# Selective-scan layer of a four-layer kernel: output gate recomputed at the end, table loads written out, bf16 remainders through the matrix engine, partial sums copied into PSUM, convolution in single taps

## The chip, the cores and the metric

The kernel runs on one core of a Trainium2 chip. The metric is the device time of one launch in microseconds (us). A core has five instruction queues that run side by side and wait for each other by semaphores: PE (TensorE, matrix products; its weight loads are listed as PEld), DVE (VectorE), ACT (ScalarE), POOL (GpSimd) and SP (SyncE, which here issues all DMAs). Each queue is strictly in order: an instruction that waits holds up everything behind it on the same queue.

## The reference, cut to what matters

Four layers follow each other on `x` of shape (8, 64, 64, 64): a state-space layer (L0), two attention layers and a test-time-training layer. Only the scan part of L0 is touched by the change. For each of the 8 images, with 64 channels, 128 inner channels (DI), 16 states (N) and 4096 positions:

```python
xz = in_proj(layernorm(x))                 # 64 -> 2*128 channels
xi, z = split(xz)
xc = silu(dwconv3x3(xi))                   # depthwise, 9 taps
xs = [rows, columns, rows reversed, columns reversed] of xc      # K = 4 directions
dts, Bs, Cs = split(xproj_w[k] @ xs[k])    # 4 + 16 + 16 rows
dt = softplus(dtproj_w[k] @ dts + dtproj_b[k])
h[n] = h[n] * exp(dt * A[n]) + dt * Bs[n] * u                    # scan over 4096 positions
y[k] = sum_n h[n] * Cs[n] + D[k] * xs[k]
y = sum of the four directions, put back in row order
out = x + outproj(layernorm(y) * silu(z))
```

## The kernel before, in words

The scan layer (`scan_layer`) is one hand-ordered program (`tc.manual_schedule()`): the engines receive instructions in the order in which the Python code emits them. For each image there are 16 **steps** (4 directions k times 4 chunks of 1024 positions), and in each step 16 **units**, one for each state n: 2048 units in all. A unit is:

- `decay` (ACT, L733): `a = exp(dt * A[n])`, 128x1024.
- `spread` (PE, L751): the row `Bs[n]`, held as three bf16 pieces (`bs`, 48 rows), is broadcast over 128 partitions into the PSUM tile `z` by two bf16 matmuls with the weights `pick`. For n in `BY_POOL = (0, 3, 6, 8)` a DMA broadcasts the row instead (`bt`), POOL multiplies it by `dt*u` (`product`, L741) and ACT copies it into `z` (L748).
- `unit` (DVE): for the other twelve n, `z = z * dt*u` (L778); then `tensor_tensor_scan` gives `h` (L782); then POOL multiplies `ct = ct * h` (L787), where `ct` is `Cs[n]` broadcast by DMA into one of five buffers.
- `sum_up` (PE, L848): `ct` is added into the PSUM tile `yps` by an fp32 matmul with a 128x128 weight, the identity or, in the last quarter of an image, the centring matrix `lno_cen` (`ident - 1/128`).

The sum runs two to three units behind (`LAG`). At n = 3, `empty` copies the finished `yps` of the step before into `y` (ACT, L817) and `begin_sum` starts the new one: in the first four steps of an image with `skipd` times u, later with the partial sum `y` itself, read back through an fp32 matmul with identity or `lno_cen` (L839). In two steps of an image the sum stays in PSUM.

Everything else is **background**: items of the form (`make`, `use`) in one queue (`Background`). Each unit takes one item (`bg.before`): `make` issues its PE work at once, `bg.after` runs what `bg.later` put off and then the `use` of the item before. In the units 6, 7, 8 (`idle`) only items without `make` are taken. Background work is:

- the normalisation and input projection of the next image (`norm_x`), its convolution (`convolve`: nine fp32 diagonal matmuls for each 512 positions, cut into items of two taps, then Silu, L553), and its gate: `gate` computes `silu(z)` and stores it in DRAM (`zd`, L529, L530);
- the layer norm of the finished image (`norm_y`: squares, variances through DRAM in `inverse_root`, root, reciprocal, then `apply`: DVE multiplies y by the row of inverse roots, L460, and ACT applies gain and bias, L461); `load` brings `zd` back (L575), POOL multiplies it with y (`multiply`, L580), and `project_out` projects and adds x;
- for the next step: `project` (step sizes dt, rows B and C) and its softplus (`soft1` to `soft3`: Exp L653, Ln L656, POOL add L659), the POOL product `step_input` (L678), and `pieces`, which splits B into three bf16 pieces: ACT rounds (L691), POOL subtracts (L695), ACT rounds the rest (L698), POOL subtracts again (L701).

Activation tables are not mentioned in the kernel; where a function is not in the loaded table, the build puts an ACT_TABLE_LOAD before the instruction that needs it, so it is shown under that instruction's line.

Of the kernel before, what the change touches and what calls it, by code (L numbers as in the profile page):

```python
# [18 lines left out]
NB = 8  # L19
# [146 lines left out]
class Background:  # L166
# [24 lines left out]
    def before(self, busy=False, slots=0):  # L191
        self.now = None
        src = None
        if busy:
            if not self.queue or self.queue[0][0]:
                return
        elif self.open:
            if not self.first and (self.item or len(self.open) >= slots or not self.queue):
                src = self.open
        elif self.groups and self.credit and not self.first and slots >= len(self.groups[0]):  # L200
            src = self.open = self.groups.popleft()
            self.credit -= 1
        if src is None and self.queue:
            src = self.queue
            self.first = max(0, self.first - 1)
        self.item = src is not self.open
        if src:
            make, use = src.popleft()
            self.now = (use, make() if make else None)
# [32 lines left out]
def scan_layer(cm, x_in, w, xh):  # L242

    tc, nc = cm.tc, cm.nc
    with ExitStack() as ctx:
# [58 lines left out]
        skipd = cm.tile([DI, DI], "skipd")  # L304
        nc.vector.tensor_scalar(skipd, cm.ident, skip, None, ALU.mult)
# [11 lines left out]
        lno_cen, lno_avg = cm.norm_consts(DI, "lno")  # L317

        eps = cm.tile([128, 1], "eps")
        nc.vector.memset(eps, 1e-5)  # L320
        pick = cm.pool.tile([3 * N, N], BF16, name="pick", tag="pick")
# [4 lines left out]
        nc.vector.tensor_copy(pick, rows)  # L326
        pad = padp.tile([DI, S + 2, S + 2], F32, name="pad", tag="pad")
        nc.gpsimd.memset(pad, 0.0)
        bg = Background()

# [5 lines left out]
        def inverse_root(nb):  # L336
# [5 lines left out]
            def put(ps, n, at):  # L342
                t = work.tile([NBK, BK], F32, name="vrow", tag="rstd", bufs=1)
# [10 lines left out]
            def root(_):  # L354
                nc.scalar.activation(sm["v"], sm["v"], AF.Sqrt, bias=eps)

# [9 lines left out]
            chain += [(None, back), none, none, none]  # L366
            return put, chain, sm

        def norm_x(b, xn, pairs, project_in):
# [48 lines left out]
            for i in pairs:  # L418
                out += [project_in(2 * i), project_in(2 * i + 1)]
                if i + 2 in pairs:  # L420
                    out.insert(-1, apply(i + 2))
                if b:
                    out.append(none)
            return out

        def norm_y(y, blocks, load, multiply, project_out):
# [8 lines left out]
            def variance(j):  # L435
# [7 lines left out]
                def use(ps):  # L443
                    put(ps, 1, j - j0)
                    if j + 2 in blocks:
                        square(j + 2)

                return make, use

            def apply(j):  # L450
# [7 lines left out]
                def use(ps):  # L458
# [3 lines left out]
                    if j - 1 in blocks:  # L462
                        multiply(j - 1)
# [4 lines left out]
            for j in blocks:  # L468
                out.append(variance(j))
                if j in blocks[1:6:2] or nb == 2:  # L470
                    at = j if nb == 2 else j0 + (j - j0) // 2
                    out.append((None, lambda _, at=at: load(at)))
            out += chain
            out += [apply(j) for j in blocks[:2]]
            end = (None, lambda _: multiply(blocks[-1]))
            if nb == 2:
                out += [end, none]
            for j in blocks:
                if j + 2 in blocks:
                    out.append(apply(j + 2))  # L480
                    if j + 2 == blocks[-1]:
                        out.append(end)
                out += [project_out(j), none]
# [5 lines left out]
        def before(b):  # L489

            xn = io.tile([2 * C, NBK // 2, BK], F32, name="xn", tag="xn", bufs=1)
# [5 lines left out]
            zd = dr.tile([DI, L], F32, name="zd", tag="zd")  # L497
# [7 lines left out]
            def project_in(j):  # L505
# [11 lines left out]

                return make, use

            def gate(j):  # L520
                def make():
                    ps = bank("zps")
                    half, x = block(j)
                    nc.tensor.matmul(ps, win[half, 1, :], x, start=True, stop=True)
                    return ps

                def use(ps):
                    z = work.tile([DI, BK], F32, name="z", tag="z", bufs=3)
                    nc.scalar.activation(z, ps, AF.Silu, bias=inb[:, 1:2])  # L529
                    bg.later(lambda: nc.sync.dma_start(zd[:, bass.ts(j, BK)], z))  # L530
# [3 lines left out]
            def convolve(j):  # L534
# [17 lines left out]
                def use(_):  # L552
                    nc.scalar.activation(u[:, bass.ts(j, BK)], held[0], AF.Silu, bias=convb)  # L553
                    if b:
                        bg.done[b] += 1

                cuts = (0, 5, 9) if b == 0 else (0, 3, 5, 7, 9) if b == NB - 1 else (0, 2, 4, 6, 8, 9)
                parts = [(part(t0, t1), None) for t0, t1 in zip(cuts, cuts[1:])]
                return parts[:-1] + [(parts[-1][0], use)]
# [4 lines left out]
            return u, zd, items, [gate(j) for j in range(NBK)], [convolve(j) for j in range(NBK)]  # L564

        def after(b, y, zd, blocks=range(NBK)):
# [4 lines left out]
            def load(j):  # L571
                xr = work.tile([C, BK], F32, name="xr", tag="xr", bufs=3)
                nc.sync.dma_start(xr, xf[:, bass.ts(j, BK)])
                z = work.tile([DI, BK], F32, name="z", tag="z", bufs=3)
                nc.sync.dma_start(z, zd[:, bass.ts(j, BK)])  # L575
                gated[j] = (xr, z)

            def multiply(j):
                z = gated[j][1]
                nc.gpsimd.tensor_tensor(z, z, y[:, bass.ts(j, BK)], ALU.mult)  # L580

            def project_out(j):
                def make():
                    po = bank("ops")
                    xr, z = gated[j]
                    nc.tensor.matmul(po[:C], cm.ident[:C, :C], xr, start=True, stop=False)
                    nc.tensor.matmul(po[:C], wout, z, start=False, stop=True)
# [12 lines left out]
            return norm_y(y, blocks, load, multiply, project_out)  # L600
# [80 lines left out]
        def pieces(ctl, low):  # L681
# [33 lines left out]
            return ([fetch, first, subtract, second, third, store] if ctl["k"] < 2 else []) + [get]  # L715
# [108 lines left out]
        def begin_sum():  # L824
# [8 lines left out]
            if ctl["new_y"]:  # L833
                wt, so = skipd, ordered(ctl["u"], ctl["k"], ctl["c"])
            else:
                mine = ("row", "col")[ctl["k"] % 2]
                wt, so = ctl["mat"], own(layout(ctl["b"], mine), ctl["c"])
            for i in range(CH // BK):
                nc.tensor.matmul(  # L839
                    ctl["ps"][:, bass.ts(i, BK)].rearrange("p (a b) -> p a b", b=S),  # L840
                    wt, so[:, i * half : (i + 1) * half, :], start=True, stop=False,
                )

        def sum_up():

            ctl, n, ct = pending.popleft()
            for i in range(CH // BK):
                nc.tensor.matmul(  # L848
                    ctl["ps"][:, bass.ts(i, BK)], ctl["mat"], ct[:, bass.ts(i, BK)],
# [19 lines left out]
        def prepare(b, s):  # L869
# [10 lines left out]
            if b == 0 and s < NCH:  # L880
# [6 lines left out]
                mat=lno_cen if s >= 3 * NCH - 1 else cm.ident,  # L887
            )
            ctl["pieces"] = pieces(ctl, low)
# [6 lines left out]
        def start(b):  # L896
            u, zd, items, gates, convs = before(b)
            images[b] = {"u": u, "zd": zd}
            bg.add(items[0] + items[1])
            if b == 0:  # L900
# [3 lines left out]
                later[NCH] = gates  # L904
            else:
                bg.done[b] = 0
                bg.add([(None, lambda _: bg.groups.extend(deque(conv) for conv in convs))])
                bg.add(gates)


        with tc.manual_schedule():
            start(0)
# [14 lines left out]
            for b in range(NB):  # L927
                for s in range(4 * NCH):
# [7 lines left out]
                    bg.credit = 2 if b == NB - 2 else 1  # L936
                    idle = () if early or late else (6, 7, 8)
                    hooks = {}
                    if nxt:
# [6 lines left out]
                        else:  # L946
                            hooks = {14 - len(do) + i: [f] for i, f in enumerate(do)}
# [10 lines left out]
                    for n in range(N):  # L958
# [30 lines left out]
                        if s == 0 and n == LAG + 2 and b > 0:  # L989
                            last = images.pop(b - 1)  # L990
                            bg.add(after(b - 1, last["row"], last["zd"]))
                            bg.add([(None, lambda _, b=b - 1: bg.flushed.add(b))])
                        if late and n == LAG + 2:
                            c = 4 * NCH - s
                            bg.add(after(b, images[b]["row"], images[b]["zd"], range(2 * c, 2 * c + 2)))
                        if s == (1 if b else NCH) and n == 0 and b + 1 < NB:
                            bg.add(later.pop(NCH, []))
# [10 lines left out]
            bg.add(after(NB - 1, last["row"], last["zd"], range(2)))  # L1008
# [1149 lines left out]
```

## Time and profile before

| | us |
|---|---|
| median of 3 runs | 12334.72 |
| lowest, highest | 12313.69, 12336.37 |
| the profiled execution itself | 12328.75 |
| its span, first to last instruction | 12326.7 |
| scan layer up to the first scan | 94.4 |
| the 2048 units of the scan layer | 94.4 to 7018.6 |
| of these, images 1 to 6 | 1015.2 to 6153.7 |
| end of the scan layer's last stores | about 7053.6 |

All numbers of the profile belong to one profiled execution. Starts of images and steps are read from the scan instructions, 16 to a step and 256 to an image. A row of a group gives busy time, mean duration in ns of one instruction, then the idle time of that engine just before it and what ended the idle time. The matrix engine's instructions overlap: an fp32 matmul is two records of about 0.6 us each, but back to back one starts every 0.43 us.

### The profile page before, as it was taken

What the parts mean: (1) busy time and instruction counts of PE and PEld (TensorE: products, weight loads), DVE (VectorE), ACT (ScalarE), POOL (GpSimd) and SP (SyncE); (2) the same over time, 40 slices, a digit from 0 to 9 for tenths busy, and PEclk for the clock granted to TensorE, in tenths of its full rate; (3) what the DMA queues carried; (4) which work ended last, traced back from release to release, by engine and by line L of the source; (5) the groups of instructions that cost most, each with busy time, mean ns of one, the idle gap of its engine ahead of it and who ended that gap; (6) DMA issues with size and microseconds to landing.
All of it is one profiled execution on the core that took longest, in us unless ns stands there. A gap on an engine that the chain in (4) does not pass through costs nothing. (4 is left out here: it accounts for less than half of the span.)

```text
span 12326.7 us, 120038 instructions
## 1 busy us (share of the span) xinstructions
PE 11203.1 (91%) x38827; PEld 4075.9 (33%) x38827; DVE 10359.2 (84%) x7334; ACT 7820.8 (63%) x10409; POOL 7399.3 (60%) x3510
## 2 busy tenths in 40 slices
PE   7899999999999999999998899999987779999999
PEld 2233332332332332333322233232335463333333
DVE  5999999999999999999999776868677686676767
ACT  4776776776766766767766554646547574555554
POOL 5999999999999999999999700000006480000000
PEclk8999999999999999999999899999998789999999
DMA  3666666666666666666666400000011100000000
GB/s 115 207 213 218 209 209 217 219 203 216 218 210 213 211 210 217 213 215 213 199 213 211 164 24 26 5 25 7 17 41 41 41 21 24 19 4 19 5 11 6
DMA packets 541331, 1562.16 MB, mean 127 GB/s; under 512 B 127360, under 2 KB 144400, under 8 KB 538128
## 3 DMA queue, kind: packets, MB, share of 16 engines
q1 hardware_dynamic: 540688, 1554.36, 38.5%
q8 instruction: 309, 5.06, 0.2%
q14 instruction: 334, 2.74, 0.1%
HBM read 1456.41 MB, written 88.87 MB: 125 GB/s over the span
## 5 line engine op out<-in xcount | busy, mean ns | idle before, releaser
L787 POOL TENSOR_TENSOR ct<-ct,h 128x1024 f32<-128x1024 f32 x2048 | 4794.6, 2364 | 248.2 <-DVE h L782 113.3
L782 DVE TENSOR_TENSOR_SCAN h<-a,state,z 128x1024 f32<-128x1024 f32 x1536 | 3573.1, 2342 | 118.2 <-ACT z L748 67.1
L1159 DVE TENSOR_TENSOR sum<-sum,ex 128x1024 f32<-128x1024 f32 x1920 | 2347.5, 1223 | 618.1 <-ACT ex L1152 484.4
L1152 ACT ACTIVATE ex<-sc 128x1024 f32<-128x1024 f32 x2048 | 1968.1, 1024 | 1359.6 <-PE sc L1147 1359.6
L848 PE MATMUL yps<-ct,ident 128*128 128x512 f32 x5632 | 2809.0, 630 | 2.5 <-POOL ct L787 2.4
L733 ACT ACTIVATE a<-dt,amat 128x1024 f32<-128x1024 f32 x2048 | 2345.4, 1147 | 725.9 <-DVE h L782 712.5
L778 DVE TENSOR_TENSOR z<-z,e 128x1024 f32<-128x1024 f32 x1536 | 1863.3, 1213 | 221.1 <-PE z L751 143.2
L1166 PE MATMUL av<-ex,v 128*64 128x512 f32 x8192 | 1950.0, 604 | 0.0
L1147 PE MATMUL sc<-q,k 16*128 16x512 f32 (+1 forms) x8192 | 1562.2, 623 | 4.2 <-ACT q L1140 3.1
L848 PEld LDWEIGHTS yps<-ct,ident 128*128 128x128 f32 x5632 | 1006.4, 194 | 1384.2 <-issue 1220.6
L751 PE MATMUL z<-bs,pick 48*128 48x512 bf16 x3072 | 948.0, 389 | 536.5 <-DVE h L782 485.5
L848 PE MATMUL yps<-ct,lno_cen 128*128 128x512 f32 x2560 | 1276.3, 630 | 0.0
L782 DVE TENSOR_TENSOR_SCAN h<-a,z 128x1024 f32<-128x1024 f32 x512 | 1162.7, 2282 | 81.4 <-ACT z L748 57.2
L741 POOL TENSOR_TENSOR bt<-bt,e 128x1024 f32<-128x1024 f32 x512 | 1210.1, 2364 | 5.3 <-DMA bt<-bc 5.3
L1473 POOL TENSOR_TENSOR gt<-gt,pad 128x1024 f32<-128x1024 f32 x16 | 34.9, 2179 | 1570.2 <-ACT gt L1472 1570.2
L1166 PEld LDWEIGHTS av<-ex,v 128*64 128x64 f32 x8192 | 512.2, 136 | 1332.8 <-issue 1278.9
L1147 PEld LDWEIGHTS sc<-q,k 16*128 16x128 f32 (+1 forms) x8192 | 528.4, 184 | 1016.2 <-issue 977.3
L748 ACT COPY z<-bt 128x1024 f32<-128x1024 f32 x512 | 519.8, 1015 | 537.5 <-POOL bt L741 334.8
L751 PEld LDWEIGHTS <-pick 48*128 48x128 bf16 x3072 | 177.6, 95 | 1754.9 <-DVE h L782 1003.0
L848 PEld LDWEIGHTS yps<-ct,lno_cen 128*128 128x128 f32 x2560 | 458.1, 193 | 618.3 <-issue 564.2
L544 PE MATMUL vps<-pad,convd 128*128 128x512 f32 x1152 | 550.9, 602 | 12.9 <-ACT e L648 12.9
L1846 DVE RECIPROCAL r<-e 128x512 f32<-128x512 f32 x128 | 420.7, 3323 | 0.0
(416 smaller groups left out, 10449.5 us busy)
## 6 DMA issues: line engine op xcount, KB each, us to landing
ct<-bc SPq DMA_DIRECT2D x2048, 512.0 KB
bt<-bc SPq DMA_DIRECT2D x512, 512.0 KB
x<-x SPq DMA_DIRECT2D x12, 2048.0 KB
bc<-e SPq DMA_DIRECT2D x128, 128.0 KB
zd<-z SPq DMA_DIRECT2D x64, 256.0 KB
z<-zd SPq DMA_DIRECT2D x64, 256.0 KB
x<-x SPq DMA_DIRECT2D x32, 512.0 KB
part<-x SPq DMA_DIRECT2D x128, 128.0 KB
```

The lines of the kernel that those rows point to most:

```text
L544: nc.tensor.matmul(held[0].rearrange("p (r c) -> p r c", c=S), convd[:, t, :], pad[:, j * rows + dy : (j + 1) * rows + dy, dx : dx + S], s ...
L733: ctl["exp", n] = nc.scalar.activation(ctl["a", n], ctl["dt"], AF.Exp, scale=amat[:, ctl["k"], n : n + 1])
L741: nc.gpsimd.tensor_tensor(bt, bt, ctl["dus"], ALU.mult)
L751: nc.tensor.matmul(z[:, bass.ts(i, BK)], pick[:, n : n + 1].to_broadcast([3 * N, DI]), ctl["bs"][:, bass.ts(i, BK)], start=True, stop=True,)
L778: first = nc.vector.tensor_tensor(z, z, ctl["dus"], ALU.mult)
L782: nc.vector.tensor_tensor_scan(h[:, flip], a[:, flip], z[:, flip], 0.0 if state is None else state[:, n : n + 1], ALU.mult, ALU.add,)
L787: freed[at] = nc.gpsimd.tensor_tensor(ct, ct, h, ALU.mult)
L848: nc.tensor.matmul(ctl["ps"][:, bass.ts(i, BK)], ctl["mat"], ct[:, bass.ts(i, BK)], start=False, stop=(n == N - 1 and not ctl["turns"]),)
L1147: nc.tensor.matmul(sc[:, e, :], k[r : r + d, bass.ts(j, 128)], qs[i][r : r + d, :], start=True, stop=True,)
L1152: nc.scalar.activation(ex, sc, AF.Exp)
L1159: nc.vector.tensor_tensor(sums[i], sums[i], ex, ALU.add)
L1166: nc.tensor.matmul(avs[i][r, :], v[:, j, r], ex[:, e, :], start=(j == 0), stop=(j == TQ - 1))
```

## The change

- **Gate.** The input block `xn` is kept (two buffers) and the gate is computed when the image is finished: the gate matmul, a Silu in place in PSUM, then a DVE multiplication into `y`. The DRAM tensor `zd`, its stores and loads, and the POOL multiplication go.
- **Remainders.** In `pieces` the two POOL subtractions (but for the first four steps) become PE matmuls: identity times B minus the pieces made so far (`rest`), rounded by ACT. The steps of `pieces` come at the units 5, 7, 8, 9, 10, 13 in place of 7 to 13, and unit 9 takes no PE item then.
- **Tables.** `exp_and_ln` loads the table set 6, which holds Exp and Ln, by hand: at the start, after each root and after each Silu. In the built program the ACT_TABLE_LOADs go from 697 to 452.
- **Variances.** The row of variances has its own two buffers (tag `vrow`, before one buffer shared with `rstd`), and one empty item leaves the chain.
- **y centred early.** Every sum uses `lno_cen`, also `skipd`. A later partial sum starts with a matmul of zeros (`nil`, one row of bf16) and ACT then copies `y` into PSUM, in place of the fp32 matmul L839.
- **Convolution.** A group opens when at least five items are left to it and is cut by what the step still offers, up to nine items of one tap; an empty item at the head of the queue gives its turn to an open group. Empty items after the projections go.

```diff
@@ Background.before
-        elif self.groups and self.credit and not self.first and slots >= len(self.groups[0]):
-            src = self.open = self.groups.popleft()
+        elif self.groups and self.credit and not self.first and slots >= 5 * self.credit:
+            src = self.open = deque(self.groups.popleft()(min(9, slots // self.credit)))
             self.credit -= 1
         if src is None and self.queue:
             src = self.queue
             self.first = max(0, self.first - 1)
+            if src[0] == (None, None) and self.open and not busy:
+                src.popleft()
+                src = self.open
@@ constants
-        nc.vector.tensor_scalar(skipd, cm.ident, skip, None, ALU.mult)
+        nc.vector.tensor_scalar(skipd, lno_cen, skip, None, ALU.mult)
+        def exp_and_ln():
+            nc.scalar.add_instruction(mybir.InstLoadActFuncSet(
+                name=nc.get_next_instruction_name(), act_func_set_id=6, engine=mybir.EngineType.Activation,
...
@@ inverse_root
-                t = work.tile([NBK, BK], F32, name="vrow", tag="rstd", bufs=1)
+                t = work.tile([NBK, BK], F32, name="vrow", tag="vrow", bufs=2)
...
                 nc.scalar.activation(sm["v"], sm["v"], AF.Sqrt, bias=eps)
+                exp_and_ln()
...
-            chain += [(None, back), none, none, none]
+            chain += [(None, back), none, none]
@@ norm_y, the order of items
-            out += [apply(j) for j in blocks[:2]]
...
+            out += [apply(j) for j in blocks[:2]] + [gate(j0)]
             for j in blocks:
                 if j + 2 in blocks:
                     out.append(apply(j + 2))
-                    if j + 2 == blocks[-1]:
-                        out.append(end)
-                out += [project_out(j), none]
+                out += [gate(j + 1) if j + 1 in blocks else none, project_out(j)]
@@ convolve
                     nc.scalar.activation(u[:, bass.ts(j, BK)], held[0], AF.Silu, bias=convb)
+                    exp_and_ln()
...
-                cuts = (0, 5, 9) if b == 0 else (0, 3, 5, 7, 9) if b == NB - 1 else (0, 2, 4, 6, 8, 9)
+                def parts(count):
...
@@ after: gate
-            def multiply(j):
-                z = gated[j][1]
-                nc.gpsimd.tensor_tensor(z, z, y[:, bass.ts(j, BK)], ALU.mult)
+            def gate(j):
+                def make():
+                    ps = bank("zps")
+                    half, x = block(j)
+                    nc.tensor.matmul(ps, win[half, 1, :], x, start=True, stop=True)
+
+                    def silu():
+                        nc.scalar.activation(ps, ps, AF.Silu, bias=inb[:, 1:2])
+                        exp_and_ln()
+
+                    bg.later(silu)
+                    return ps
+
+                def use(ps):
+                    v = y[:, bass.ts(j, BK)]
+                    nc.vector.tensor_tensor(v, ps, v, ALU.mult)
@@ pieces
+            def rest(i):
+                def do():
+                    ps = bank("brps")
+                    b, p = (low[n] for n in "bp")
+                    nc.tensor.matmul(ps[:, :256], cm.ident, b.rearrange("p a x -> p (a x)"), start=True, stop=False)
+                    for q in range(i):
+                        nc.tensor.matmul(
+                            ps[:, :256], minus, p[:, q].rearrange("p a x -> p (a x)"),
+                            start=False, stop=(q == i - 1),
+                        )
+                    nc.scalar.copy(p[:, i].rearrange("p a x -> p (a x)"), ps[:, :256])
...
-            return ([fetch, first, subtract, second, third, store] if ctl["k"] < 2 else []) + [get]
+            return [fetch, first, rest(1), rest(2), store, get]
@@ begin_sum
-                wt, so = ctl["mat"], own(layout(ctl["b"], mine), ctl["c"])
+                y = layout(ctl["b"], mine)
+                for i in range(CH // BK):
+                    nc.tensor.matmul(
+                        ctl["ps"][:, bass.ts(i, BK)], nil, nil[:, :1].to_broadcast([1, BK]), start=True, stop=False
+                    )
+                bg.later(lambda: nc.scalar.copy(ctl["ps"], y[:, bass.ts(ctl["c"], CH)]))
+                return
@@ sum_up
-                    ctl["ps"][:, bass.ts(i, BK)], ctl["mat"], ct[:, bass.ts(i, BK)],
+                    ctl["ps"][:, bass.ts(i, BK)], lno_cen, ct[:, bass.ts(i, BK)],
@@ main loop
-                    bg.credit = 2 if b == NB - 2 else 1
-                    idle = () if early or late else (6, 7, 8)
+                    bg.credit = 2 if b == NB - 2 and len(bg.groups) > 4 * NCH - 1 - s else 1
+                    parts = nxt and not early and nxt["k"] < 2
+                    idle = () if early or late else (6, 7, 8, 9) if parts else (6, 7, 8)
...
-                            hooks = {14 - len(do) + i: [f] for i, f in enumerate(do)}
+                            hooks = dict(zip((5, 7, 8, 9, 10, 13) if parts else (13,), ([f] for f in do)))
```

## The prediction

> **What bounds the kernel now.** I read the page first, for where the time lies, then busy time by stretch, then the groups of POOL, DVE and ACT inside six images, then a few microseconds of ACT in order of time.
>
> ```profile
> span 12326.7 us, 120038 instructions
> PE 11203.1 (91%) x38827; PEld 4075.9 (33%) x38827; DVE 10359.2 (84%) x7334; ACT 7820.8 (63%) x10409; POOL 7399.3 (60%) x3510
> DVE  5999999999999999999999776868677686676767
> POOL 5999999999999999999999700000006480000000
> ```
>
> POOL's 60% is an average: it is full for the first 57% of the span, the scan layer, and nearly empty after. Only this stretch changes. Its busy time:
>
> ```profile
> core 0: us, PE busy (x) PEld busy (x) DVE busy (x) ACT busy (x) POOL busy (x), PEclk, DMA share, GB/s
> 1015.20:6153.70 5138.50, 4769.09 (x10962) 1627.69 (x10962) 4912.30 (x2774) 3694.35 (x5291) 5015.75 (x2257) 0.97 0.65 213
> 6640.70:6692.50 51.80, 44.01 (x100) 14.51 (x100) 50.78 (x29) 32.75 (x50) 51.80 (x25) 0.97 0.66 220
> 374.10:432.40 58.30, 49.25 (x111) 16.84 (x111) 50.21 (x30) 55.00 (x67) 51.25 (x23) 0.91 0.65 207
> ```
>
> The first row is images 1 to 6: POOL is busy 97.6%, DVE 95.6%, PE 92.8%. The second is a step without background work: POOL is busy for all of its 51.80 us, DVE for 50.78. So POOL is the bound, and DVE stands only 2% behind. The third is step 4 of image 0, where all eight gates are computed: ACT is nearly full and the step is 58.3 us.
>
> ```profile
> L787 POOL TENSOR_TENSOR ct<-ct,h 128x1024 f32<-128x1024 f32 x1537 | 3597.7, 2363 | 122.8 <-DMA ct<-bc 49.9 <-DVE h L782 46.1 <-PE z L751 13.1
> ...
> L580 POOL TENSOR_TENSOR z<-z,y 128x512 f32<-128x512 f32 x48 | 61.2, 1276 | 0.0
> L701 POOL TENSOR_TENSOR bp<-br,bp 128x256 bf16<-128x256 f32 x48 | 32.3, 673 | 0.0
> L695 POOL TENSOR_TENSOR br<-bw,bp 128x256 f32<-128x256 f32 x48 | 32.3, 672 | 0.0
> ```
>
> The last three rows are what the change takes from POOL. POOL's whole idle time is 122.8 us in 5138.5.
>
> ```profile
> L782 DVE TENSOR_TENSOR_SCAN h<-a,state,z 128x1024 f32<-128x1024 f32 x1153 | 2682.3, 2342 | 83.7 <-ACT z L748 46.4 <-POOL ct L787 6.0
> L778 DVE TENSOR_TENSOR z<-z,e 128x1024 f32<-128x1024 f32 x1152 | 1397.3, 1213 | 122.1 <-PE z L751 76.2 <-POOL ct L787 21.2 <-ACT state L769 6.9
> L782 DVE TENSOR_TENSOR_SCAN h<-a,z 128x1024 f32<-128x1024 f32 x385 | 874.3, 2282 | 20.4 <-POOL ct L787 10.0 <-ACT z L748 0.3
> L460 DVE TENSOR_TENSOR y<-y,rps 128x512 f32<-128x512 f32 x48 | 31.7, 661 | 0.0
> ```
>
> DVE idles 83.7 + 122.1 + 20.4 = 226 us, for three neighbours: PE's spread (76), ACT's copy of POOL's product (46), POOL itself (37). The rest is mostly small gaps, some 0.02 us at each of 2,690 instructions, about 50 us.
>
> ```profile
> L344 ACT COPY vrow<-vps 1x512 f32<-1x512 f32 x48 | 27.5, 573 | 73.0 <-DMA vard<-vrow 67.0 <-PE vps L438 5.9
> L698 ACT CAST bp<-br 128x256 bf16<-128x256 f32 x48 | 19.4, 405 | 141.3 <-POOL br L695 141.1
> L748 ACT COPY z<-bt 128x1024 f32<-128x1024 f32 x384 | 389.8, 1015 | 405.3 <-POOL bt L741 273.3 <-DVE h L782 111.6 <-DVE z L778 12.6
> ```
>
> ACT is not full, but it is in order: while it waits 141 us for POOL's remainders and 67 us for a DMA to release `vrow`, the decays and copies behind it stand still.
>
> **The change, part by part.**
>
> *POOL* (images 1 to 6): minus 48 x 1.276 = 61.2 (gate) and 96 x 0.673 = 64.6 (remainders), together 126: 5016 becomes 4890.
>
> *DVE*: plus 48 multiplications of a PSUM by an SBUF operand, 128x512. L460 is the same operation: 0.661 each, 31.7 in all: 4912 becomes 4944. DVE is now the fuller engine, so the new time is 4944 plus its waits.
>
> *PE*: the readback L839 of y goes (320 records in the whole layer, at 0.43 us back to back: 138). It adds 80 pairs of zero matmuls (a pair of L751, also bf16 with 512 columns, takes 0.60: 48), and for 60 chunks two fp32 matmuls of 256 columns and three bf16 ones: between 0.21 and 0.43 a record for 240 records and 0.11 to 0.30 for 180, so 70 to 157; near half of the 512-column rows, 80. Net about -10, hidden in PE's idle 7%. What counts is how the work is spread. Per unit, DVE needs about 3.5 us (1.21 + 2.34, slightly overlapped). PE needs 0.60 (spread) + 4 x 0.43 (sum) = 2.3; with two taps (4 records, 1.72) 4.0, with one tap 3.2. Two taps make the next spread late, one doesn't. Summing PE's work per unit along the built instruction order, with these durations: 55 units in an image exceed 3.35 us, by 22 us in all; after, 31 by 7 us. That takes DVE's wait for PE from 76 to between 76 x 7/22 = 24 and 76 x 31/55 = 43. I take 28.
>
> *ACT*: 246 table loads fewer in the scan layer (545 to 299, counted in the built order) x 1.283 = 316 us. It adds 80 copies of y into PSUM; L748 is the same copy, 1.015: 81. The two waits above go: in `rest` ACT waits for one PE item instead, and with two `vrow` buffers the second variance need not wait for the DMA. All of this lies beside DVE; what it buys is that z arrives in time. On PE, `rest` waits for ACT's piece of one unit earlier, with the next spread behind it; ACT has then had 3.5 us for a copy of 0.4, so nothing, at most 0.5 us x 120. DVE's 46 us wait for ACT's z I put at 15, between 0 and 46, because POOL's product, which ACT awaits longest (273 us), is also earlier.
>
> The new copy of y waits for the zero matmul, and the first sum waits for the copy. Behind that sum on PE is the spread of the next unit but one (unit 6 needs none), so DVE doesn't feel it; behind it on SP is the load of a `ct` buffer, which needs the sum. Before, the sum waited for L839 instead (1.9 us); now for a decay, a state copy and the copy, 1.15 + 0.17 + 1.02 = 2.3 us. Cost 0.4 us, which the double sum at unit 7 absorbs: nothing, at most 1 us x 80 (rival 2).
>
> *The gate's path and its tables.* Two switches surround each Silu. The trace:
>
> ```profile
> 3019.33 1.28 ACT L656 ACT_TABLE_LOAD   x1
> 3020.63 1.06 ACT L656 ACTIVATE e<-e 128x1024 f32<-128x1024 f32 x1
> ```
>
> A switch is 1.28 us, and the next instruction starts 0.02 us later. The Trainium skill ("ScalarE: Activation LUTs", What ACT_TABLE_LOAD costs) gives about 2.66 us for each switch, load and drain, and advises to do all calls of one set before changing, which speaks against switching twice around every 512 positions. From the rows: gate matmul done 0.60 + 1.72 + 0.86 = 3.2 us into the unit, switch and Silu (0.69, row L529) end at 5.2; DVE comes to the multiplication after the following unit, at 7.0, or 5.8 if that unit has no L778. It does not wait. With 2.66 the Silu ends at 6.6, and 64 gates would wait up to 0.8 us: 51 us more. I go by the trace, and keep the 51 for the range.
>
> *SP*: 64 stores and 64 loads of `zd` fewer, about 0.4 and 0.6 us of issue each. SP mostly waits for sums to free `ct`; no gain. The earlier fetch of B (unit 5) waits on SP for a landed store; the tables ahead had slack of units, so nothing, at most 0.5 us x 60.
>
> *DVE's waits after*: PE 28, ACT 15, POOL 37 to 8 (it has 54 us less work than DVE now), small gaps 50, together 101. Images 1 to 6: 4944 + 101 = 5045, a change of -94.
>
> *Edges.* Before the first scan: two table loads on the chain to the first step size (2.6) and one `vrow` wait (1.3): -4. Step 4 of image 0 loses its gates: 58.3 to about 52.3: -6. Its other late steps (583 us), in proportion: -10. Image 7, steps 0 to 12 (693 us, DVE 664): 664 + 5 + 14 = 683: -10. Its last three steps and the tail: two items go into one unit, so DVE waits for Silu behind two switches, about 2 us in each step, plus 2 x 0.66; in the tail two switch pairs stand on the chain of the output, +3: together +13. The first four steps are cut as before: 0.
>
> Sum: -94 - 4 - 6 - 10 - 10 + 13 = -111, from 12328.75 to 12218. The profiled execution is 6 us below the median of the three runs, inside their spread of 23; I round to 12215.
>
> **The rivals.** *1, DVE's waits collapse.* If PE's, ACT's and POOL's waits were all echoes of POOL's load, only the small gaps stay: 4944 + 50 = 4994, 51 us further: 12165; without the edge losses 12150. For it: steps of 50.2 us with DVE at 49.7 exist. Against: PE still has 31 crowded units an image.
>
> *2, late sums.* The copy of y finds ACT behind its decays, the sum is late, the `ct` load and POOL follow: POOL already waits 49.9 us for `ct`. At 1 us x 80: about 12295.
>
> *3, slower: DVE was the real bound.* Then POOL's 97.6% only follows DVE, its relief buys nothing, and every added microsecond on DVE counts. Price: 64 x 0.661 = 42, with DVE's waits unchanged, +13 at the end, -10 at the start: +45, 12375; with the 51 of late Silus 12425. It decides if less than about 45 us of DVE's waits in the layer vanish. Against: the quiet step with POOL full and DVE idle for 1 us.
>
> **How the numbers follow.** The sum as worked out 0.62, rival 1 0.18, rival 2 0.11, rival 3 0.09. About 0.2% (25 us) is what a measurement of this kernel can tell from no change. Faster: the sum, rival 1 and two thirds of rival 2: 0.86; same 0.06, slower 0.08. The range runs from rival 1 with some more on ACT, 12130, to just beyond rival 2, 12310.
>
> **What would show it.** Right: in images 1 to 6 DVE above 97% and above POOL; POOL rows L580, L695, L701 gone but for four chunks; DVE's wait for PE's z about halved; no ACT wait on `vrow` or remainders. Wrong: DVE waiting for ACT at the gate's multiplication; POOL's wait for `ct` DMAs well over 50 us; DVE's total wait still above 200 us.

## The result and the profile after

The changed kernel takes 12227.74 us, median of 4 runs (12221.52 to 12237.85); the kernel before took 12330.01 beside it. The ratio is 0.9919 with a 95% interval of 0.9907 to 0.9931: about 100 us faster. The profiled execution took 12228.28 us.

The page of the changed kernel, the lines that answer to those shown of before:

```profile
span 12226.5 us, 120204 instructions
...
PE 11196.6 (92%) x39087; PEld 4103.2 (34%) x39087; DVE 10380.4 (85%) x7400; ACT 7575.7 (62%) x10304; POOL 7247.3 (59%) x3326
...
DVE  4999999999999999999999776868778676676767
...
POOL 4999999999999999999999500000007480000000
```

POOL has lost 152 us of work and ACT 245, the span 100. Busy time by stretch in the changed kernel: images 1 to 6, a step with convolution only, a step full of gates, then image 7 up to step 12 and its last three steps.

```profile
core 0: us, PE busy (x) PEld busy (x) DVE busy (x) ACT busy (x) POOL busy (x), PEclk, DMA share, GB/s
...
1002.30:6053.00 5050.70, 4766.22 (x11160) 1649.16 (x11160) 4923.82 (x2821) 3509.41 (x5210) 4899.09 (x2113) 0.97 0.64 211
2370.40:2422.50 52.10, 51.38 (x124) 18.78 (x123) 50.88 (x30) 36.03 (x55) 51.19 (x23) 0.97 0.64 215
4520.80:4578.40 57.60, 55.26 (x125) 17.39 (x124) 54.93 (x37) 44.32 (x63) 50.83 (x22) 1.00 0.59 199
6053.00:6747.70 694.70, 610.74 (x1383) 202.22 (x1383) 666.77 (x382) 447.88 (x676) 662.78 (x287) 0.95 0.62 208
6747.70:6915.80 168.10, 152.54 (x338) 49.32 (x338) 160.54 (x100) 121.13 (x176) 147.89 (x64) 0.94 0.56 187
```

PEclk is the TensorE clock that was granted, as a share of full speed. Images 1 to 6 took 5138.5 us and now take 5050.7, 88 less, at the same granted clock of 0.97. DVE (97.5% busy) has passed POOL (97.0%). Steps of convolution stand near 52 us, but a step full of gates takes 57.6 with DVE at 54.9. That is where time was lost again. The groups of DVE in images 1 to 6 (three small ones left out):

```profile
L811 DVE TENSOR_TENSOR_SCAN h<-a,state,z 128x1024 f32<-128x1024 f32 x1153 | 2680.0, 2341 | 50.6 <-ACT z L777 18.5
L807 DVE TENSOR_TENSOR z<-z,e 128x1024 f32<-128x1024 f32 x1152 | 1394.4, 1210 | 47.0 <-PE z L780 23.7 <-ACT u L543 5.0 <-ACT e L639 4.7
L811 DVE TENSOR_TENSOR_SCAN h<-a,z 128x1024 f32<-128x1024 f32 x384 | 870.9, 2281 | 23.2 <-ACT z L777 12.4 <-POOL ct L816 0.6
L589 DVE TENSOR_TENSOR y<-zps,y 128x512 f32<-128x512 f32 x48 | 32.1, 670 | 6.2 <-ACT zps L581 5.8
```

DVE's idle time is 127 us, after 226: the wait for PE's z fell from 76 to 24, that for POOL nearly to nothing, that for ACT's z only from 46 to 31. L589 is the new gate product, 670 ns.

One of ACT's waits that were to go has only changed its cause. Before, ACT waited 141.1 us for POOL's remainders; now it waits for those of PE, in images 1 to 6 (total, times, longest):

```profile
ACT bp L736 <- PE brps L732: 132.2, 92, 2.7
```

Where ACT's z still comes late is seen at a gate, in the changed kernel's ACT and then DVE in order of time (start, duration, in brackets the idle time before and who ended it):

```profile
4538.34 1.28 ACT L581 ACT_TABLE_LOAD   x1 [3.88 <-PE zps L578]
4539.64 0.66 ACT L581 ACTIVATE zps<-zps,inb 128x512 f32<-128x512 f32 x1
4540.31 1.28 ACT L340 ACT_TABLE_LOAD   x1
4541.61 0.81 ACT L476 ACTIVATE y<-y,on_b,on_g 128x512 f32<-128x512 f32 x1
4542.33 1.00 ACT L777 COPY z<-bt 128x1024 f32<-128x1024 f32 x1
```

```profile
4540.52 0.67 DVE L589 TENSOR_TENSOR y<-zps,y 128x512 f32<-128x512 f32 x1
4543.43 2.35 DVE L811 TENSOR_TENSOR_SCAN h<-a,state,z 128x1024 f32<-128x1024 f32 x1 [2.24 <-ACT z L777]
```

ACT stood 3.88 us with the table load at its head, waiting for the gate's matmul; load, Silu, load and an affine followed, and the copy of z behind them ended 2.24 us after DVE wanted it. The gate's own multiplication did not wait here.

### The profile page after: what moved, and what is told of

Its sections match the earlier page's. It is cut to its first block, busy times and chain, and to the rows that moved or that the text cites. A ratio compares the mean times of both kernels' runs of the same rounds, so it can differ in the third digit from the quotient of the medians.

```text
span 12226.5 us, 120204 instructions
## 1 busy us (share of the span) xinstructions
PE 11196.6 (92%) x39087; PEld 4103.2 (34%) x39087; DVE 10380.4 (85%) x7400; ACT 7575.7 (62%) x10304; POOL 7247.3 (59%) x3326
## 5 line engine op out<-in xcount | busy, mean ns | idle before, releaser
L882 PE MATMUL yps<-ct,lno_cen 128*128 128x512 f32 x8192 | 4119.9, 633 | 58.6 <-ACT yps L869 57.2
L882 PEld LDWEIGHTS yps<-ct,lno_cen 128*128 128x128 f32 x8192 | 1476.4, 195 | 2078.9 <-issue 1818.0
L1881 POOL TENSOR_TENSOR r<-r,half 128x512 f32<-128x512 f32 x128 | 162.7, 1271 | 361.9 <-issue 186.0
L798 ACT COPY state<-h 128x1 f32<-128x1 f32 x2048 | 362.9, 177 | 0.0
```

The costliest lines, as they stand in the source:

```text
L882: nc.tensor.matmul(ctl["ps"][:, bass.ts(i, BK)], lno_cen, ct[:, bass.ts(i, BK)], start=False, stop=(n == N - 1 and not ctl["turns"]),)
```

## The experiments

Each kernel is timed beside the kernel before, whose median was 12326, 12325 or 12322 us there. For comparison with the changed kernel (0.9919) the ratios are used; a difference of two such ratios is sure to about 0.002, some 25 us, so that the differences of 23 us stand at the edge of what can be told. No run has the new gate alone, nor the `vrow` buffers or the early centring.

| kernel | median us | ratio to before, 95% | against the changed kernel, or before, us |
|---|---|---|---|
| before, half of `step_input` | 12272.12 | 0.9956 (0.9943 to 0.9970) | before -54 |
| changed, half of `step_input` | 12214.74 | 0.9909 (0.9894 to 0.9924) | -12 |
| changed, two taps | 12249.34 | 0.9938 (0.9924 to 0.9951) | +23 |
| changed, tables by the build | 12233.89 | 0.9921 (0.9907 to 0.9935) | +2 |
| changed, remainders on POOL | 12270.46 | 0.9952 (0.9938 to 0.9965) | +41 |
| changed, idle POOL load | 12251.46 | 0.9945 (0.9931 to 0.9958) | +32 |
| changed, gate product on POOL | 12217.60 | 0.9911 (0.9897 to 0.9924) | -10 |
| changed, gate matmul first | 12200.93 | 0.9896 (0.9881 to 0.9911) | -28 |
| changed, both of these | 12205.73 | 0.9905 (0.9890 to 0.9920) | -17 |
| changed, readback of y on PE | 12198.24 | 0.9900 (0.9885 to 0.9915) | -23 |
| before, single taps only | 12356.87 | 1.0023 (1.0016 to 1.0031) | before +28 |
| before, remainders on PE only | 12315.85 | 0.9994 (0.9986 to 1.0002) | before -7 |

**Was POOL the bound, and is it still?** The same edit in both kernels:

```diff
-            nc.gpsimd.tensor_tensor(ctl["dus"], ctl["dt"], ctl["ut"]["u"], ALU.mult)
+            nc.gpsimd.tensor_tensor(
+                ctl["dus"][:, : CH // 2], ctl["dt"][:, : CH // 2], ctl["ut"]["u"][:, : CH // 2], ALU.mult
+            )
```

> The kernel before, with step_input multiplying only the first half of dt*u (128x512 in place of 128x1024; the second half of that product is left out). POOL saves about 2.36 - 1.27 = 1.09 us in each of 128 steps, 140 us; no other engine waits directly for this product, which is ready units ahead. Theory (POOL was the bound before): the time falls by 80 to 140 us, to 12190 to 12250. Rival (DVE was the bound and POOL only followed it): no change beyond 25 us, 12305 to 12355.

> The changed kernel with the same half left out of dt*u: POOL again saves 140 us. Theory (the bound has passed from POOL to DVE): it falls by less than 40 us, 12190 to 12228. Rival (POOL is still the bound): it falls by 80 to 140 us, to 12090 to 12150.

In the kernel before, some 140 us less of POOL buy 54; in the changed kernel 12. POOL is the bound no longer, as expected, but it never was alone: neither the theory's 80 nor the rival's nothing came in the kernel before. That the bound is now DVE is read from its 97.5%; no run takes work off DVE alone. Images 1 to 6 of before with half the product, and DVE's longest waits there (total, times, longest):

```profile
1014.60:6102.80 5088.20, 4727.67 (x10962) 1616.42 (x10962) 4906.58 (x2773) 3694.25 (x5291) 4915.60 (x2257) 0.98 0.65 215
```

```profile
DVE z L780 <- PE z L753: 56.2, 56, 3.3
DVE h L784 <- ACT z L750: 43.2, 22, 4.4
```

POOL fell by 100 us, the stretch by 50. DVE's wait for PE fell by 20, that for ACT's z (46.7 before) hardly: most of these two did not hang on POOL. A part of the 50 us may have come by another way: the granted clock was 0.98 in these images against 0.97, and 0.954 to 0.956 over the timed runs against 0.951 to 0.954 of the kernel before. No run separates the two.

**Two taps again, and tables left to the build.**

```diff
-            src = self.open = deque(self.groups.popleft()(min(9, slots // self.credit)))
+            src = self.open = deque(self.groups.popleft()(min(5, slots // self.credit)))
```

> The changed kernel with the convolution cut into at most five items of two taps, as before. Theory (a unit with two taps needs 4.0 us of PE against 3.5 of DVE, so the next spread is late): DVE's waits for PE come back from 24 to 60 to 80 us in images 1 to 6, and the time rises by 40 to 65 us, to 12268 to 12293. Rival (the waits for PE were only an echo of a full POOL): within 15 us of 12228.

Between theory and rival: +23 us. DVE's wait for PE's z in images 1 to 6 rises from 23.7 to

```profile
DVE z L807 <- PE z L780: 40.7, 49, 2.6
```

not to 60. Images 1 to 6 take 5067.1 us, 16 more, about what DVE waits more for PE (17). Two taps in a unit do make the next spread late, but cost about half of what was expected; why the rest is absorbed was not tested.

For the second run, `exp_and_ln` does nothing.

> The changed kernel without the table loads written out: the build puts a load wherever the loaded table lacks the function, so Exp and Ln change tables in every step again, about 0.3 ms more of ACT work. Theory (ACT has room, 850 us of waiting for DVE in images 1 to 6, and only some copies of z come later): 10 to 50 us slower, 12238 to 12278. Rival (the table loads were a main part of the gain): 80 us slower or more, above 12308.

Neither: +2 us, within the uncertainty. Images 1 to 6 take 10 us more:

```profile
998.90:6059.60 5060.70, 4780.96 (x11160) 1649.72 (x11160) 4930.10 (x2821) 3756.86 (x5396) 4898.33 (x2113) 0.97 0.64 211
```

ACT has 247 us more to do (3756.86 against 3509.41) and the launch is not measurably longer. In the changed kernel the decays alone had waited 850 us for DVE. DVE's wait for ACT's z at the scan did not grow: it is 13.1 us, 30.9 in the changed kernel. In its place DVE waits longer for PE's z (31.8) and at the gate's product (10.2).

**The remainders: POOL's time or ACT's wait for POOL?** First `pieces` with the POOL subtractions, then PE's remainders kept and two POOL instructions added that nobody reads:

```diff
-            ctl["pieces"] = pieces(ctl, low, b == 0 and s < NCH)
+            ctl["pieces"] = pieces(ctl, low, True)
...
-                            hooks = dict(zip((5, 7, 8, 9, 10, 13) if parts else (13,), ([f] for f in do)))
+                            hooks = dict(zip((5, 7, 8, 9, 10, 11, 13) if parts else (13,), ([f] for f in do)))
```

> The changed kernel with the two remainders subtracted on POOL again, at the new places (units 8 and 10): POOL gets back 60 x 1.35 = 81 us. Theory (POOL and DVE are now nearly level, 4899 and 4924 us busy in images 1 to 6, so that 65 us more puts POOL ahead again): 20 to 45 us slower, 12248 to 12273. Rival (POOL now has slack, and the remainders cost nothing there): within 10 us of 12228.

```diff
+            def idle_pool(last):
+                def do():
+                    t = work.tile([128, 2, 128], F32, name="br", tag="br", bufs=1)
+                    nc.gpsimd.tensor_tensor(t, low["b"], low["b"], ALU.subtract)
+                    last()
...
-            return [fetch, first, rest(1), rest(2), store, get]
+            return [fetch, first, idle_pool(rest(1)), rest(2), idle_pool(store), get]
```

> The changed kernel with two idle POOL subtractions of 128x256 put in at units 8 and 10 of the same steps; nothing reads what they write, and the remainders stay on PE and ACT. It separates the two things that the run with the remainders back on POOL (12270) changed at once. Theory (the 81 us of POOL time are what counts): 20 to 45 us slower than 12228, 12248 to 12273. Rival (ACT's wait for POOL's differences, 167 us there, was what made it slower): at most 12 us slower, below 12240.

Both as the theory had it: +41 and +32. Images 1 to 6 of the two, and DVE's wait for POOL in the second, 0.6 us in the changed kernel:

```profile
1010.60:6100.50 5089.90, 4729.82 (x10824) 1600.38 (x10822) 4931.66 (x2820) 3494.88 (x5162) 4957.56 (x2210) 0.97 0.63 210
```

```profile
1008.90:6089.10 5080.20, 4783.10 (x11160) 1650.88 (x11160) 4932.91 (x2821) 3508.63 (x5210) 4952.07 (x2209) 0.97 0.63 210
```

```profile
DVE h L819 <- POOL ct L824: 24.6, 37, 1.1
```

Against 5050.7 that is 39 and 30 us, at the same granted clock of 0.97: three quarters of the cost is POOL's time, without anyone waiting for a difference. The rest may be ACT's wait (166.7 us for POOL's differences in the first run); the difference of the two runs is too small to tell.

**Parts of the change alone.** In the kernel before, only the cutting of the convolution and its turn in the queue; then only `rest` with the new places and the idle unit 9.

> The kernel before with only the convolution changed: groups cut into up to nine items of one tap, and empty items give way to an open group; everything else as before. In the built order the crowded units fall from 55 to 23 in an image, but the queue runs late, and three output projections fall into one unit of step 5 (7.7 us of PE). Theory (POOL is full, so that PE's crowded units are in good part hidden): 0 to 25 us faster, 12300 to 12326. Rival (PE's crowding was what made the time): 40 us faster or more.

The rival is refuted and the theory too: 28 us slower. Steps 4 and 5 of one image in this run, then PE and DVE in order of time within step 5:

```profile
2933.50:2986.70 53.20, 51.81 (x117) 16.52 (x116) 52.43 (x34) 34.27 (x52) 53.20 (x26) 0.97 0.70 237
2986.70:3055.10 68.40, 63.62 (x124) 19.11 (x122) 51.91 (x30) 39.63 (x60) 56.05 (x26) 0.83 0.60 184
```

```profile
3003.95 1.97 PE L597 MATMUL ops<-z,wout 128*64 128x512 f32 x2
3005.85 1.97 PE L596 MATMUL ops<-xr,ident 64*64 64x512 f32 x2
3007.74 1.97 PE L597 MATMUL ops<-z,wout 128*64 128x512 f32 x2
```

```profile
3010.88 1.23 DVE L788 TENSOR_TENSOR z<-z,e 128x1024 f32<-128x1024 f32 x1 [11.34 <-PE z L761]
```

Step 5 takes 68.4 us (53.0 on average before). Output projections come in one burst, and DVE waits 11.34 us for the spread behind them. The granted clock of the step is only 0.83, and the records of the burst start every 0.95 us instead of 0.43; how much of the 15 us is the burst and how much the clock is not separated. This step alone explains the loss: over images 1 to 6 it takes 90 us more than before, and all other steps together 55 less. Why the projections come in a burst was not tested by itself. The likeliest reading: nine items for each group leave the queue no room, so that they are late when `y` needs its buffer. In the changed kernel the same cutting may fit because eight gates have left the queue's middle and the empty items behind the projections are gone.

> The kernel before with only the remainders moved to PE and ACT, at the places and with the idle unit of the changed kernel. POOL saves 81 us and ACT no longer waits 141 us for POOL in images 1 to 6; PE gets some 80 us more. Theory (this is the largest single part of the change): 35 to 60 us faster, 12267 to 12292. Rival (the gain needs the gate and the taps as well, because PE stays crowded): less than 15 us faster, above 12312.

The rival: 7 us, no difference that can be told. In this run DVE's wait for PE and POOL's for its operand are, in images 1 to 6 (before: 76.2 and 49.9):

```profile
DVE z L798 <- PE z L771: 88.9, 96, 4.3
```

```profile
POOL ct L807 <- DMA ct<-bc: 100.7, 91, 3.9
```

POOL has 57 us less to do (4958.6), but nearly all of it came back as waits. The likely chain: PE, with 61 us more to do beside its two-tap units, sums later, and `ct` is loaded later; SP's wait for the sums is 3787.5 us, 3633.8 before.

**What is left of the gate.** First the gate's matmul ahead of the sums, then its product on POOL, then both:

```diff
+                            soon = n not in idle and bg.queue and getattr(bg.queue[0][0], "soon", False)
+                            if soon:
+                                bg.before(n in idle, slots)
                             if len(pending) > LAG:
                                 sum_up()
...
-                            bg.before(n in idle, slots)
+                            if not soon:
+                                bg.before(n in idle, slots)
```

> The changed kernel with the gate's matmul issued ahead of the sums of its unit, so that it ends about 1.7 us earlier. In the changed kernel ACT stands 70 us in images 1 to 6 waiting for this matmul, and the copies of z behind it make DVE wait 31 us. Theory (this queueing on ACT is what is left of the gate's cost): 10 to 30 us faster, 12198 to 12218. Rival (the sums come later instead, and with them the ct loads that POOL waits for): within 10 us of 12228 or slower.

28 us faster, inside the theory's range, but not where it was expected: in images 1 to 6 only 4 us (5046.4). DVE's waits there:

```profile
DVE z L808 <- PE z L781: 42.0, 43, 2.4
DVE h L812 <- ACT z L778: 10.8, 13, 1.6
```

(23.7 and 30.9 in the changed kernel.) The step full of gates behaves as the theory had it, 55.2 us for 57.6 in each of the six images, 14 us in all. Other steps took 10 back. The first two rows are the step full of gates and step 7 of one image in this run, the third is the same step 7 in the changed kernel:

```profile
1999.70:2054.90 55.20, 53.89 (x125) 17.27 (x124) 54.77 (x36) 44.69 (x63) 50.76 (x22) 1.00 0.66 210
2217.40:2274.40 57.00, 55.25 (x119) 18.44 (x119) 52.14 (x32) 38.51 (x60) 51.30 (x23) 0.88 0.58 190
```

```profile
2215.30:2268.80 53.50, 51.86 (x119) 17.75 (x119) 52.01 (x31) 38.49 (x60) 51.21 (x22) 0.94 0.61 203
```

Step 7 was granted a clock of 0.88 here and 0.94 there, and its 119 matmuls took 55.25 us of PE for 51.86. So the longer wait for PE goes with the clock; whether the edit changed the clock is not shown. Image 7 gains 14 us, 862.8 to 848.6, in the steps of gates and in step 0; step 0 was granted a clock of 1.00 instead of 0.91.

```diff
+                    z = work.tile([DI, BK], F32, name="zs", tag="sq")
...
-                        nc.scalar.activation(ps, ps, AF.Silu, bias=inb[:, 1:2])
+                        nc.scalar.activation(z, ps, AF.Silu, bias=inb[:, 1:2])
...
-                    return ps
+                    return z
...
-                    nc.vector.tensor_tensor(v, ps, v, ALU.mult)
+                    nc.gpsimd.tensor_tensor(v, z, v, ALU.mult)
```

> The changed kernel with the gate's product on POOL again: Silu writes an SBUF tile and POOL multiplies it into y (64 x 1.27 = 81 us more on POOL, 64 x 0.67 = 43 less on DVE); no detour through DRAM. Theory (POOL becomes the fuller engine again, 4960 against 4892 us): 10 to 35 us slower, 12238 to 12263. Rival (only DVE's load counts now): 20 to 43 us faster, 12185 to 12208.

10 us faster, within the uncertainty: neither theory nor rival. DVE and POOL are so level that taking 43 us from the one and giving 81 to the other comes out even. Beside the run with the idle POOL load it also tells what DVE's time is worth: in images 1 to 6 POOL is busy for 4955.6 and 4952.1 us, DVE for 4896.2 and 4932.9, and the stretch takes 5043.3 and 5080.2. With POOL alike, 37 us less of DVE went with 37 us less of time; but the two runs differ in the kind of POOL work as well.

> The changed kernel with both edits that came out faster: the gate's matmul ahead of the sums of its unit (12201 alone) and the gate's product on POOL from an SBUF tile (12218 alone). Theory (the first removes ACT's late copies of z, the second takes 43 us from DVE, which is the bound): together 30 to 45 us below 12228, 12183 to 12198. Rival (with 81 us more, POOL holds it again): not below 12201.

The rival: together not better than the first alone.

**The readback of y.** `begin_sum` as before, with the identity in place of the zero matmuls and the copy.

```diff
-                        ctl["ps"][:, bass.ts(i, BK)], nil, nil[:, :1].to_broadcast([1, BK]), start=True, stop=False
+                        ctl["ps"][:, bass.ts(i, BK)].rearrange("p (a b) -> p a b", b=S),
+                        cm.ident, own(y, ctl["c"])[:, i * half : (i + 1) * half, :], start=True, stop=False,
...
-                bg.later(lambda: nc.scalar.copy(ctl["ps"], y[:, bass.ts(ctl["c"], CH)]))
```

> The changed kernel with the partial sum read back into PSUM by an fp32 matmul with the identity again, in place of zero matmul and ACT copy: 80 x 1.7 us more on PE, at unit 3, which then holds 3.2 us of PE work, still under DVE's 3.5. Theory (where this unit has room it costs nothing): within 10 us of 12228. Rival (PE is close enough to full that 138 us of it count): 30 us slower or more, above 12258.

23 us faster: neither theory nor rival. Images 1 to 6 take 5027.9 us, 22.8 less, and practically all of it lies there. In the changed kernel the first sum waits for the copy in 59 of 60 steps:

```profile
PE yps L882 <- ACT yps L869: 44.0, 59, 0.9
```

That this late sum is the cost does not hold. PE from the start of a partial sum to the first `ct` added to it, in the same step of the changed kernel and of this run:

```profile
2279.61 0.60 PE L866 MATMUL yps<-nil 1*128 1x512 bf16 x2
2280.19 0.59 PE L780 MATMUL z<-bs,pick 48*128 48x512 bf16 x2
2281.46 1.96 PE L882 MATMUL yps<-ct,lno_cen 128*128 128x512 f32 x4 [0.68 <-ACT yps L869]
```

```profile
2276.92 1.88 PE L866 MATMUL yps<-y,ident 128*128 128x512 f32 x4
2278.73 0.60 PE L780 MATMUL z<-bs,pick 48*128 48x512 bf16 x2
2279.26 1.98 PE L882 MATMUL yps<-ct,lno_cen 128*128 128x512 f32 x4
```

With the copy the first sum comes 1.85 us after the start, without it 2.34; over the 60 partial sums of images 1 to 6 the means are 1.9 and 2.4. The wait of 0.68 us is shorter than the matmuls that it replaces, and both steps take 50.1 us.

What does differ is the granted clock: 0.99 in images 1 to 6 against 0.97, and 0.958 to 0.959 in all four timed runs against 0.951 to 0.952 of the changed kernel. What a lower clock costs is seen inside one execution. Step 4 of two images in the changed kernel, then in this run:

```profile
2057.70:2111.70 54.00, 48.09 (x108) 15.57 (x108) 51.65 (x32) 36.26 (x52) 50.71 (x22) 0.97 0.69 215
3737.70:3795.60 57.90, 52.84 (x108) 16.92 (x108) 52.05 (x33) 36.25 (x52) 50.06 (x22) 0.88 0.60 197
```

```profile
3729.00:3783.00 54.00, 48.09 (x108) 15.52 (x108) 51.65 (x33) 36.26 (x52) 50.74 (x22) 0.97 0.65 211
```

The same 108 matmuls keep PE busy for 48.09 us at 0.97 and 52.84 at 0.88, and the step is 3.9 us longer. The longer one has a wait of DVE for a Silu that the shorter one does not have:

```profile
3760.23 0.69 DVE L589 TENSOR_TENSOR y<-zps,y 128x512 f32<-128x512 f32 x1 [2.75 <-ACT zps L581]
```

Where the clock is alike, the steps of the two kernels are alike: 54.0 us in step 4, 57.6 in the step full of gates, 50.1 in step 8. So the 23 us go with the clock. Why this kernel was granted more of it in every execution stays open. The edit is the only difference between the programs, and two other variants of the changed kernel that were timed beside it, the idle POOL load and both gate edits, were granted 0.951 to 0.953. POOL's wait for the `ct` DMA fell too, from 51.0 to 31.6 us; whether as cause or effect is not shown.

This and the gate's matmul first are the two fastest kernels tried; they were not run together.

## Why the prediction was right, and which terms were off

- **Total.** 12215 forecast, 12227.74 measured; a gain of 111 in the sum, 100 in the spans. The likeliest case held, and the range. That it came so close is in part luck: in images 1 to 6 DVE's work was put 20 us too high and its waits 26 too low, and the errors at the edges cancel as well.
- **Images 1 to 6.** -94 forecast, -88 measured. The bound passed to DVE as worked out: DVE 4944 forecast and 4923.8 measured, POOL 4890 and 4899.1. DVE's own increase is 11.5 us, not 31.7. The rows of its groups add up to 23.5 us more: 32.1 for the new product, less 8.6 because the other instructions are 1 to 3 ns shorter and one scan fewer falls into the stretch. Another 12 lie over the ends of neighbouring instructions, so that they add no busy time.
- **DVE's waits.** 101 forecast, 127 measured. PE 28 and 23.7: right. POOL 8 and 4: right. ACT's z 15 and 34 (30.9 at the scan, 3.4 at the product): the mis-sized term. The step that put it at 15 gave credit to the removed table loads, to two ACT waits that were to go, and to POOL's earlier product. The product did come earlier (ACT's wait for it fell from 273 to 51 us) and the wait for `vrow` went, but that for the remainders stayed (141 and 132). In the run without hand-written loads ACT has 247 us more work and DVE's wait for z at the scan is 13.1, so fewer loads were not what shortens this wait. The run with the gate's matmul first shows that most of the wait stands behind the gates (31 falls to 11).
- **The gate's path.** "It does not wait": nearly so, 5.8 us in 3 of 48 gates, 2.75 of them in the step at a clock of 0.88. What was overlooked is who stands behind the Silu on ACT: the copy of z for DVE. On the tables the trace was right, and the 2.66 us of the Trainium skill ("ScalarE: Activation LUTs", What ACT_TABLE_LOAD costs) too much: 4540.31 + 1.28 and the next instruction at 4541.61. The advice to do all calls of one set before changing stands in the same page under "Table sets: the hidden batching unit"; here 236 switches more cost nothing that can be told.
- **The copy of y.** "Nothing, at most 1 us x 80": nothing is what the steps of equal clock show, but not for the reason given. The sum was to be 0.4 us later than behind the readback, 2.3 against 1.9 us, and a double sum was to absorb it; in the step shown it is 0.5 us earlier (1.85 against 2.34). The run without the copy was 23 us faster at a higher clock, a term that the prediction doesn't have. Rival 2 did not come: POOL's wait for `ct` is 51.0 us, 49.9 before.
- **Edges.** Before the first scan -3.2 (forecast -4). Step 4 of image 0 58.3 to 52.7 (-6 forecast), its later steps 583 to 571 (-10 forecast): right. Its first four steps 279.7 to 287.0, forecast 0: wrong; the granted clock was 0.90 against 0.91, and no run here tells more. Image 7 to step 12: 693.4 to 694.7, forecast -10: wrong. Its gate steps took back what POOL's relief gave, and so did step 0, which ran at a clock of 0.91; with the gate's matmul first the image is 14 us shorter, 4.5 of them in step 0 at a clock of 1.00. Last three steps 171.5 to 168.1, forecast slower by 10: wrong, the two errors cancel.
- **Rivals.** Rival 1 did not come: DVE still waits 127 us, not 50. Rival 3 fell: less work for POOL alone, in the kernel before, is worth 54 us of 140, though some of that may be clock. That DVE stands close behind, as rival 3 has it, is one limit on it.

The gain is not a sum over parts. Single taps alone cost 28 us, remainders alone give 7; yet taking one of them out of the whole costs 23 or 41. The likely reason, which no run isolates, is that each makes the room that the other needs: time on PE in a unit, and turns in the background queue.

## What to carry to other kernels

Where three engines are above 90%, as here, the work taken off the first is an upper limit of the gain: 100 us less of POOL gave 50. Take some work off the first without touching anything else, and measure that before moving work. A background item is not cheap because its engine has room: ask what stands behind it on that engine's queue, and whose next instruction that is. Before cutting work finer, count the turns it needs. And before a difference of some 20 us is put down to an edit, compare the granted clock of the two runs, stretch by stretch.

## What was not expected of the hardware

In these kernels 236 table loads of 1.283 us, 303 us of ACT time, could be removed or left in with a difference of 2 us: ACT, 74% busy in images 1 to 6 with them and waiting for DVE most of the rest, takes them whole. And within one execution the same step of the same kernel takes 54.0 or 57.9 us, with a granted TensorE clock of 0.97 or 0.88, although DVE, not PE, is the fullest engine. Two kernels that differ only in how a partial sum is put into PSUM were granted 0.951 to 0.952 and 0.958 to 0.959 in all their executions, and that went with a difference of 23 us.
